# Layer 1 of a four-layer convolution kernel with three engines in fixed order, layer 2's first weights made in layer 0, and the last statistics from sums of two terms

## The chip, the cores and the metric

The kernel runs on one core of one Trainium2 chip. The metric is device time in microseconds (us) of one execution of the whole program. Every figure for a kernel is a median of its runs; beside it stands the range. Each result was correct against the reference. A submission runs its kernels and the kernel before in turn on one chip, so ratios are taken inside a submission: a ratio is the mean time of one kernel's fast runs over that of the other's of the same rounds, so it is not quite the ratio of the medians that are quoted.

In the lines of the profiler and in the recorded texts PE is TensorE (the matmuls), PEld its weight loads, DVE VectorE, ACT ScalarE and POOL GpSimd; L574 is line 574 of the kernel. A hole is idle time of TensorE between two matmuls. A half-clock stretch is a piece, 3.41 us or twice that unless said otherwise, in which the trace shows the granted TensorE clock at 0.50.

## The reference, cut to what matters

Input is x of 16 images, 256 channels, 28 x 28 pixels (784 per image and channel), in float32. Four layers follow each other.

```python
# layer 0: y = batchnorm(conv3x3(sign(x), sign(w))) + x            (statistics over all images)

# layer 1, per image, no statistics over images inside:
residual = prelu(x, a_alpha1)
z  = sign(x + a_move)
y  = prelu(bn(conv3x3(z, a_w)), a_alpha2)
g  = sigmoid(relu(mean(s*x + (1-s)*y) @ w1.T + b1) @ w2.T + b2)    # gate: one number per channel
y  = bn(g * y * residual) + residual
u  = prelu(bn(conv1x1(sign(y + f_move), f_w)), f_alpha2)
g2 = sigmoid(relu(mean(s2*y + (1-s2)*u) @ w1'.T + b1') @ w2'.T + b2')
x  = bn(g2 * u) + y

# layer 2 begins with statistics of that x over ALL images and pixels:
m, v = mean(x), var(x)
out  = sign(batchnorm(x))        # then conv3x3 with sign(w1) * mean(|w1|), and so on
# ... (rest of layer 2)
# layer 3: attention over the 784 pixels of each image, plus x
```

Two things matter. In layer 1 each image has a chain: 3x3 convolution, gate, product, 1x1 convolution, second gate, sum. Only the images are independent of each other. And layer 2 can't begin before the last image's x is in its statistics.

Of the kernel before, what the change touches and what calls it, by code (L numbers as in the profile page):

```python
# [64 lines left out]
def conv_seq_kernel(ctx: ExitStack, tc: tile.TileContext, d: dict, out: bass.AP):  # L65
# [78 lines left out]
    def norm(name, moments, gamma, beta, sf=None):  # L144
# [14 lines left out]
        r = rsqrt(name, v, half)  # L159
        tt(c, m, r, ALU.mult)  # L160
# [27 lines left out]
    def sign_weights(pool, dst, src, total, acc, stage=("st", 2), spare_dve=False, tmp=None, ab_tag="rn"):  # L188
# [9 lines left out]
        def sign(k, g):  # L198
            st = sts[k, g]
            n = CHUNKS.index((k, g))  # L200
            if n == 5:
                A.activation(dst[1], st, AF.Sign, saturate=False)
                return
            sg = tmp.tile([P, 3, 256], BF16, tag="t1", name="sg", bufs=2)
            A.activation(sg, st, AF.Sign, saturate=False)
            V.scalar_tensor_tensor(dst[0][:, n], sg[:, :, P:], PACK, sg[:, :, 0:P], ALU.mult, ALU.add)  # L206

        def add_up(k, g):
            st = sts.pop((k, g))
            if spare_dve:  # L210
                ab = st[:, 0, :]
                A.activation(st, st, AF.Abs)
                nc.gpsimd.tensor_tensor(ab, ab, st[:, 1, :], ALU.add)
                nc.gpsimd.tensor_tensor(ab, ab, st[:, 2, :], ALU.add)
            else:
                ab = tmp.tile([P, 256], F32, tag=ab_tag, name="ab", bufs=4 if ab_tag == "rn" else 2)
                V.tensor_reduce(ab, st.rearrange("p t o -> p o t"), AX.X, ALU.add, apply_absolute_value=True)
# [116 lines left out]
    with tc.tile_pool(name="ps_conv", bufs=3, space=PSUM) as psc, \  # L334
# [13 lines left out]
        with tc.tile_pool(name="ph1", bufs=1) as ph:  # L348
# [47 lines left out]
            def w1_step(k, c):  # L396
                sts = []

                def load():
                    sts.append(ph.tile([P, 3, 256], F32, tag="st", name="st", bufs=2))  # L400
# [18 lines left out]
            def fw_step():  # L419
                sts = []  # L420

                def load():
                    sts.append(ph.tile([P, 3, 256], F32, tag="st", name="stf", bufs=2))
# [46 lines left out]
            steps = load_ahead(steps, 2) + [x.work for x in sums_] + [constants]  # L470
# [17 lines left out]
            sc0, bi0 = norm("l0", mom, pv("g0"), pv("b0"), sf0)  # L488
            zb1 = tt(vtile("zb1"), bi0, pv("a_move"), ALU.add)
            nbi0 = combine("nbi0", bi0, -1.0)  # L490
            tt(mix_c[:, 0], pv("a_scale"), bi0, ALU.mult)

# [43 lines left out]
            def enter(b):  # L536

                sx = sums_of(b + 1)[0][:, 0]
                for k in range(2):
                    x = xs[b][:, k, :]  # L540
                    V.scalar_tensor_tensor(
                        x, ns[b][:, k, :], sc0[:, k:k + 1], x, ALU.mult, ALU.add, accum_out=sx[:, k:k + 1]
                    )
                    A.activation(inner(pads[b % 2], k), img(x), AF.Sign, bias=zb1[:, k:k + 1], saturate=False)

            def transform(b):
# [4 lines left out]
                terms = (  # L551
                    (e0, e1, ALU.subtract), (o0, e1, ALU.add), (e1, o0, ALU.subtract), (o0, o1, ALU.subtract)
                )
                for pair in ((1, 2), (0, 3)):
                    for k in range(2) if b == 0 else (slice(0, 2),):
                        for u in pair:
                            x, y, op = terms[u]
                            tt(vs[:, b % 2, u, k], x[:, k], y[:, k], op)

            def residual(b):  # L560

                for k in range(2):
                    x = xs[b][:, k, :]
                    r = relu_neg(x, nbi0[:, k:k + 1])
                    V.scalar_tensor_tensor(x, r, ra1[:, k:k + 1], x, ALU.mult, ALU.add)  # L565
# [15 lines left out]

            ys, us = {}, {}
# [7 lines left out]
            def sum_pair(b, mo):  # L590

                ps = pairs.pop((b, mo, True))
                t1, uv = temp("t1"), ph.tile([P, 2, HN], F32, tag="uv", name="uv", bufs=2)
                A.activation(t1, ps[:, 0, :HN], AF.Identity, bias=c1[:, mo:mo + 1], scale=s1[:, mo:mo + 1])
                for i, s in enumerate((s1, ns1)):
                    V.scalar_tensor_tensor(uv[:, i], ps[:, 1, :HN], s[:, mo:mo + 1], t1, ALU.mult, ALU.add)  # L596
                pairs[b, mo] = uv

            def rows_out(b, mo):
                ps = pairs.pop((b, mo, False))  # L600
                uv = pairs.pop((b, mo))
# [8 lines left out]
                pairs[b, mo] = relu_neg(y)  # L610

            def prelu_out(b, mo):
# [6 lines left out]
            def gates_hidden(t):  # L619
# [5 lines left out]
                tt(p, p, r, ALU.add)  # L625
                h = hidden[t % 3]
                for g, ps in enumerate(hidden_sums(p)):
# [15 lines left out]
            def branch1_a(b, g):  # L643
                for k in range(2):
                    y = ys[b, k]
                    if b == B - 1 and k == 1:
                        V.tensor_scalar(y, y, g[:, k:k + 1], 1.0, ALU.mult, ALU.add)
                    else:
                        A.activation(y, y, AF.Identity, bias=ones, scale=g[:, k:k + 1])

            def branch1_b(b):

                sv = sums_of(b + 2)[0][:, 1]
                room_x2(b)
                z2[b] = ph.tile([P, 2, N], FR, tag="z2", name=f"z2_{b}", bufs=1)
                for k in range(2):
                    v = x2[b][:, k, :]
# [696 lines left out]
```

## The kernel before: the parts that the change touches

Channels lie on the 128 partitions in two halves (`k` for input, `mo` for output). The 3x3 convolution of layer 1 is made of four products per pair of rows (`u` from 0 to 3), each of 12 matmuls. `conv_ps()` gives one of three PSUM buffers in rotation. Only TensorE's order is fixed by hand; VectorE and ScalarE are ordered by a scheduler that takes the order of the program text as a priority.

```python
with tc.manual_schedule(engines={ET.PE}):
    for b in range(B + 2):
        now, one, two, ahead = b < B, 0 <= b - 1 < B, 0 <= b - 2 < B, b + 1 < B
        if now:
            for i, u in enumerate((1, 2)):
                conv_pair(b, 0, i, u)            # TensorE: 24 matmuls
        ...
        if one or two:
            h = gates_hidden(b)                  # gate of b-1, second gate of b-2: "hid" on TensorE
        if now:
            sum_pair(b, 0)
            conv_pair(b, 0, 0, 0)
        if ahead:
            enter(b + 1)                         # next x: n * scale + x, and its signs
        if one or two:
            g = gates(h)                         # "gate" on TensorE
        if now:
            conv_pair(b, 0, 1, 3)
        ...
        if one:
            branch1_a(b - 1, g[:, 0])            # y * gate + 1
            branch1_b(b - 1)                     # times residual; z = its signs
        if now:
            rows_out(b, 0)                       # frees a PSUM buffer
        if two:
            branch2(b - 2, g[:, 1])              # x = u * gate + v, sums, squares, store
        if now:
            for i, u in enumerate((1, 2)):
                conv_pair(b, 1, i, u)
            prelu_out(b, 0)
        ...
        if ahead:
            transform(b + 1)                     # sums of rows for the next image's products
        if one:
            conv1x1(b - 1)                       # TensorE: 16 matmuls, two PSUM buffers
        if late:
            late()                               # a step that makes weights of layer 2
        if now:
            sum_pair(b, 1)
            for i, u in enumerate((0, 3)):
                conv_pair(b, 1, i, u)
        if one:
            unit_a(b - 1)                        # reads the result of the 1x1 convolution
        if ahead:
            residual(b + 1)
        if now:
            rows_out(b, 1)
        if one:
            unit_b(b - 1)                        # its sum is an input of the next "hid"
        if now:
            prelu_out(b, 1)
        late = steps.pop(0)() if b >= 2 and steps else None
```

The weights of layers 0 and 2 are used as signs, packed two to a number, and a matmul with a column of ones ("sumabs") gives the mean of their absolute values. One step does both:

```python
def sign(k, g):
    ...
    sg = tmp.tile([P, 3, 256], BF16, tag="t1", name="sg", bufs=2)
    A.activation(sg, st, AF.Sign, saturate=False)
    V.scalar_tensor_tensor(dst[0][:, n], sg[:, :, P:], PACK, sg[:, :, 0:P], ALU.mult, ALU.add)

def add_up(k, g):                       # the other form, on ScalarE and GpSimd, is cut
    st = sts.pop((k, g))
    ...
    V.tensor_reduce(ab, st.rearrange("p t o -> p o t"), AX.X, ALU.add, apply_absolute_value=True)
    return lambda: total_up(k, g, ab)   # 4 "sumabs" matmuls on TensorE, one step later

def both(first, second):
    return [Step(f.load, lambda f=f, s=s: (f.work(), s.work())[1]) for f, s in zip(first, second)]
```

After the last image, `moments1` adds up `sum_x2` and `sum_sq`, the sums of x and of (x + shift) squared per image, and only then does layer 2's scale and shift follow. `keep_busy(n)` issues n matmuls whose result is not used, so that TensorE's clock stays up.

## Time and profile before

| | before |
|---|---|
| median of 3 runs, us | 1184.69 (1183.12 to 1186.47) |
| layer 0 ends (TensorE's last product) | 157.7 |
| start of layer 1 | 7.5 |
| loop of layer 1, first product to last | 390.3 |
| tail: to the first product of layer 2 | 26.4 |
| first half image of layer 2 | 6.9 |

The rows of the table come from the starts of TensorE's instructions in the trace; they cut the time a little differently from the prediction's stages. The execution of before that was profiled took 1187.65 us, more than any of the three runs in the table.

On the page of the kernel before, these are the chain of work that ended last (share of the span by engine) and the group of the layer 1 products (busy time and mean ns of one, then the idle time of the engine just ahead of them and what ended most of it):

```profile
PE 62%; DVE 16%; ACT 4%; issue 2%; DMA 2%; DVEq 0%; ACTq 0%
L573 PE MATMUL cv<-vs,w 128*128 128x392 f32 x1536 | 309.9, 361 | 8.3 <-ACT rn L533 6.8
```

TensorE is busy nearly all the time, yet only 62% of the chain runs through it, and 16% through VectorE: in part of the program TensorE is led by others. The products' own idle time is small, 8.3 us. The larger idle time stands in front of the tiny gate matmuls, and the prediction shows it.

### The profile page before, as it was taken

The page shows a single profiled execution, that of the slowest core. Times are in us where ns is not written, and L with a number is a line of the kernel's source. Part 1 is how long each engine was busy: PE and PEld are TensorE (multiplying, and loading weights), DVE is VectorE, ACT ScalarE, POOL GpSimd, SP SyncE. Part 2 cuts the span into 40 slices and gives each one's busy share as a digit, 9 for nine tenths or more (in the row PEclk, how much of TensorE's full clock was granted, in tenths as well). Part 3 has the DMA queues.
Part 4 walks back from the last instruction along what each step waited for, and adds up shares of the span by engine and source line. Part 5 has one row for each costly group of instructions (what it writes and reads, how often), then busy time and mean ns, then how long its engine had stood idle before and what let it go on. Part 6 is the DMA issues. An engine that isn't in the chain of part 4 may idle for free.

```text
span 1185.9 us, 15794 instructions
## 1 busy us (share of the span) xinstructions
PE 1129.0 (95%) x6069; PEld 954.7 (81%) x6075; DVE 794.7 (67%) x1410; ACT 714.2 (60%) x1053; POOL 146.0 (12%) x144
## 2 busy tenths in 40 slices
PE   6999999998999999999999999999999999999995
PEld 6999989988999999998699998999965555555542
DVE  3854378888788888865476665666673666676565
ACT  4644545666667766755655554555567667767742
POOL 2000000011010000000000000000004434424421
PEclk9999999999999999999999999999999999999998
DMA  7653431222223212100545000000002554554522
GB/s 283 205 170 124 139 108 55 82 82 82 82 85 106 83 69 77 60 28 28 217 150 215 1 1 1 1 1 1 1 28 82 137 146 108 156 154 114 141 82 84
DMA packets 25973, 111.63 MB, mean 94 GB/s; under 512 B 3554, under 2 KB 6308, under 8 KB 25892
## 3 DMA queue, kind: packets, MB, share of 16 engines
q1 hardware_dynamic: 20436, 80.85, 19.4%
q0 software_dynamic: 5456, 29.71, 8.7%
q8 instruction: 50, 0.82, 0.3%
q14 instruction: 31, 0.25, 0.1%
HBM read 65.59 MB, written 44.96 MB: 93 GB/s over the span
## 4 chain that ended last, share of the span: by engine, by line
PE 62%; DVE 16%; ACT 4%; issue 2%; DMA 2%; DVEq 0%; ACTq 0%
PE cv L252 20%; PE cv L573 12%; PE sc L1014 7%; PE av L1035 6%; PE mi L999 4%; PE sm L1075 4%; DVE vs L103 2%; PE unused L346 2%; PE cv L271 2%; PE mi L1085 2%; PE cv L670 2%; DMA xs<-in_x_dram 2%; DVE y L606 2%; DVE uv L596 2%; DVE xs L565 1%
## 5 line engine op out<-in xcount | busy, mean ns | idle before, releaser
L573 PE MATMUL cv<-vs,w 128*128 128x392 f32 x1536 | 309.9, 361 | 8.3 <-ACT rn L533 6.8
L252 PE MATMUL cv<-fpads,wpk 128*128 128x392 f32 x1440 | 294.3, 357 | 10.9 <-DVE wpk L206 9.9
L573 PEld LDWEIGHTS cv<-vs,w 128*128 128x128 f32 x1536 | 293.0, 194 | 13.5 <-ACT rn L533 9.5
L252 PEld LDWEIGHTS cv<-fpads,wpk 128*128 128x128 f32 x1440 | 272.2, 192 | 15.7 <-issue 8.9
L1018 ACT ACTIVATE es<-sc 112x784 f32<-112x784 f32 x112 | 87.3, 821 | 74.7 <-PE sc L1014 74.5
L850 DVE SCALAR_TENSOR_TENSOR p<-r,r,cv 128x392 f32<-128x392 f32 x128 | 78.6, 614 | 79.7 <-ACT r L847 79.7
L252 PE MATMUL cv<-fpads,wpl 128*128 128x392 f32 x576 | 124.8, 352 | 0.0
L252 PEld LDWEIGHTS cv<-fpads,wpl 128*128 128x128 f32 x576 | 108.8, 190 | 0.6
L263 ACT ACTIVATE t<-cv,rounding 128x392 f32<-128x392 f32 x96 | 56.2, 585 | 87.2 <-PE cv L252 84.8
L1014 PE MATMUL sc<-q,k 64*112 64x392 f32 x448 | 90.4, 518 | 2.2 <-DVE k L1006 1.5
L264 DVE TENSOR_SCALAR uv<-t 128x392 fp32r<-128x392 f32 x96 | 35.0, 364 | 82.8 <-ACT t L263 82.8
L847 ACT ACTIVATE r<-cv 128x784 f32<-128x784 f32 (+1 forms) x66 | 52.9, 804 | 60.1 <-PE cv L271 59.2
L1035 PE MATMUL av<-es,va 112*64 112x392 f32 x448 | 80.8, 499 | 0.0
L1014 PEld LDWEIGHTS sc<-q,k 64*112 64x112 f32 x448 | 36.4, 175 | 43.6 <-issue 18.7
L1028 POOL TENSOR_TENSOR sum<-sum,es 112x784 f32<-112x784 f32 x32 | 68.4, 2139 | 2.5
L1035 PEld LDWEIGHTS av<-es,va 112*64 112x64 f32 x448 | 29.6, 136 | 47.4 <-issue 44.6
L103 DVE TENSOR_TENSOR vs<-pad 128x840 fp32r<-128x840 bf16 (+1 forms) x68 | 65.3, 985 | 2.4 <-PE cv L573 1.5
L1006 DVE COPY k<-mi 64x784 f32<-64x784 f32 x16 | 15.6, 976 | 65.1 <-ACT q L1005 65.1
L477 ACT CAST n<-cv 128x784 int16<-128x784 f32 x32 | 26.0, 812 | 55.1 <-DVE l_parts L476 24.2
L1075 PEld LDWEIGHTS sm<-wv,p 128*112 128x112 f32 x448 | 46.7, 178 | 5.0 <-issue 2.6
L1089 DVE TENSOR_TENSOR p<-mi,p 128x784 f32<-128x784 f32 x30 | 29.2, 974 | 31.5 <-PE mi L1085 31.1
L271 PE MATMUL cv<-uv,unpack 128*128 128x392 f32 x192 | 49.9, 341 | 0.0
(235 smaller groups left out, 1669.1 us busy)
## 6 DMA issues: line engine op xcount, KB each, us to landing
xs<-in_x_dram SPq DMA_DIRECT2D x32, 784.0 KB, 4.6
x2d<-x POOLq DMA_DIRECT2D x16, 784.0 KB, 3.8
xd<-p SPq DMA_DIRECT2D x16, 784.0 KB, 3.3
out_dram<-p SPq DMA_DIRECT2D x15, 784.0 KB, 5.2
p<-x2d SPq DMA_DIRECT2D x13, 784.0 KB, 7.6
p<-x2d POOLq DMA_DIRECT2D x13, 784.0 KB, 9.1
n0d<-n POOLq DMA_DIRECT2D x16, 392.0 KB, 2.7
n<-n0d SPq DMA_DIRECT2D x16, 392.0 KB, 3.1
```

The lines of the kernel that those rows point to most:

```text
L103: V.tensor_tensor(o, a, b, op)
L252: T.matmul(pss[j][:, mo, :HN].rearrange("p (a b) -> p a b", b=S), lhsT=lhsT, rhs=pads[:, j // 2 % 2, k, r:r + HR, c:c + S], start=start, s ...
L263: A.activation(r, pss[j][:, 0, :HN], AF.Identity, bias=rounding, scale=1.0 / PACK)
L271: T.matmul(pss[j][:, mo, :HN], lhsT=unpack[mo], rhs=bs[j], start=False, stop=True, skip_group_check=(mo == 0))
L573: T.matmul(ps.rearrange("p (a b) -> p a b", b=S), lhsT=w[:, k, c, u, mo * P:(mo + 1) * P], rhs=vs[:, b % 2, u, k, :, c:c + S], start=(n == 0),
L847: A.activation(r[:, mo], ps[:, mo, :HN], AF.Relu, scale=-1.0)
L850: V.scalar_tensor_tensor(p, r[:, mo], beta[:, mo:mo + 1], ps[:, mo, :HN], ALU.mult, ALU.add)
L1014: T.matmul(ps[:MC, h, :HN], lhsT=k_[rows, c * MC:(c + 1) * MC], rhs=qs[b][rows], start=True, stop=True)
L1018: A.activation(e, ps[:MC, :, :HN], AF.Exp, scale=0.125)
L1028: (V if late else nc.gpsimd).tensor_tensor(sums[b, late], sums[b, late], e, ALU.add)
L1035: T.matmul(ps[64 * h:64 * h + 64, :HN], lhsT=w, rhs=e[:, h, :], start=start, stop=stop)
L1075: T.matmul(ps[:MC, c * 64:(c + 1) * 64], lhsT=x[b][:, k, c * MC:(c + 1) * MC], rhs=wv[:, k, :], start=(k == 0), stop=(k == 1),)
```

## The change

Three things are done together.

1. **Layer 1.** VectorE and ScalarE get a fixed order too, not only TensorE. The iteration is cut elsewhere: the gate's two matmuls stand one product later, the 1x1 convolution stands at the end of TensorE's iteration, and the passes that read its result move to the start of the next iteration. So does the second prelu.
2. **Layer 2's first weights** (five steps of signs, packing and absolute sums) are made in layer 0, whose VectorE and ScalarE have room, and no longer in layer 1. They get buffers of their own. The other weight steps of layer 0 are spread out between them.
3. **The tail.** For the last image, x = v + g u. Its sum and its sum of squares are formed from sums of v and u before the gate g is known, so the two passes that make x no longer stand ahead of the shift and scale of layer 2. The load of the square root's table is pulled ahead.

The diff is long; this is its core, with cuts marked by "...".

```diff
-            sg = tmp.tile([P, 3, 256], BF16, tag="t1", name="sg", bufs=2)
+            sg = tmp.tile([P, 3, 256], BF16, tag="sg", name="sg", bufs=1)
...
-            steps = load_ahead(steps, 2) + [x.work for x in sums_] + [constants]
+            w2a = [packed_weights(wpool, tag="wa2"), None]
+            signs2, sums2 = sign_weights(xpool, w2a, d["w2a"], sf1, pss, ("x2", 3), tmp=ph)
+            steps = load_ahead(steps + both(signs2, sums2)[:5], 2)
+            for i, x in enumerate(sums_):
+                steps.insert(2 * i + 1, x.work)
+            steps.insert(13, constants)
...
-            with tc.manual_schedule(engines={ET.PE}):
-                for b in range(B + 2):
...
+            def iteration(b):
+                ahead, one, two = b + 1 < B, b >= 1, b >= 2
...
+                for i, u in enumerate((1, 2)):
+                    conv_pair(b, 0, i, u)
+                if two:
+                    unit_u(b - 2, 0)
+                if one:
+                    prelu_a(b - 1, 1)
+                if two:
+                    unit_r(b - 2, 0)
+                    unit_u(b - 2, 1)
+                    unit_r(b - 2, 1)
...
+                conv_pair(b, 0, 0, 0)
+                h = hidden_a(b) if one else None
...
+                if one:
+                    h = hidden_b(b, h)
...
+                conv_pair(b, 0, 1, 3)
+                rows_out(b, 0)
+                if one:
+                    g = gates(h)
...
+                for i, u in enumerate((1, 2)):
+                    conv_pair(b, 1, i, u)
...
+                if ahead:
+                    transform(b + 1, 0)
+                    transform(b + 1, 3)
+                    for i, u in enumerate((0, 3)):
+                        conv_pair(b, 1, i, u)
+                    rows_out(b, 1)
+                    if one:
+                        conv1x1(b - 1)
...
+            with tc.manual_schedule(engines={ET.PE, ET.DVE, ET.Activation}):
+                sc0, bi0 = norm("l0", mom, pv("g0"), pv("b0"), sf0, first)
...
+                squares(x2[b][:, 0, :], shift[:, 0:1], sum_vv[:, 0:1])
...
+                for k in range(2):
+                    products(x2[b][:, k, :], shift[:, k:k + 1], us[b, k][0], sum_uv[:, k:k + 1])
+                squares(us[b, 0][0], 0.0, sum_uu[:, 0:1])
...
+                def moments1():
+                    tt(d1, su, g, ALU.mult)
+                    tt(q1, sum_uu, g, ALU.mult)
...
+                sg1, bg1 = norm("l2a", moments1, pv("g1"), pv("b1"))
+                for k in range(2):
+                    branch2(b, k, g)
...
-            keep_busy(20)
-            sg1, bg1 = norm("l2a", moments1, pv("g1"), pv("b1"))
+            keep_busy(12)
```

## The prediction

> **What bounds the kernel now.** I read the page's totals first, then the table of stages, then who waits for whom in layer 1, then one iteration in order of time.
>
> ```profile
> PE 1129.0 (95%) x6069; PEld 954.7 (81%) x6075; DVE 794.7 (67%) x1410; ACT 714.2 (60%) x1053; POOL 146.0 (12%) x144
> ```
>
> TensorE is the fullest engine, but that row is an average over stages. The table of stages (length, busy time and count of PE, weight loads, DVE, ACT, POOL, granted clock, DMA share, GB/s) splits it:
>
> ```profile
> 13.00:158.00 145.00, 143.81 (x751) 141.13 (x753) 73.69 (x190) 73.89 (x121) 8.32 (x15) 1.00 0.48 168
> 158.00:165.20 7.20, 6.50 (x31) 2.80 (x31) 5.48 (x22) 3.20 (x6) 0.54 (x1) 1.00 0.44 135
> 165.20:366.00 200.80, 185.05 (x961) 181.16 (x962) 167.09 (x312) 131.75 (x182) 13.53 (x16) 0.96 0.24 81
> 366.00:555.80 189.80, 181.19 (x961) 175.25 (x961) 151.01 (x285) 124.16 (x177) 5.41 (x12) 0.99 0.18 63
> 555.80:581.90 26.10, 23.31 (x107) 12.32 (x107) 15.12 (x44) 14.44 (x25) 2.11 (x6) 0.93 0.22 81
> 581.90:717.00 135.10, 133.67 (x715) 131.76 (x716) 84.83 (x167) 75.78 (x99) 0.00 (x0) 1.00 0.29 113
> ```
>
> Layer 0 (13 to 158) and layer 2 (from 582) are PE streams without holes. Layer 1 (165.2 to 555.8, 390.6 us) has PE holes, DVE is over 80% busy there, and the clock is below 1. The stage after it, the tail of layer 1, takes 26 us in which PE mostly runs filler. Who waits for whom in layer 1 (total, times, longest):
>
> ```profile
> PEld hid L507 <- DVE g L103: 21.3, 14, 2.7
> PE hid L507 <- DVE g L103: 16.7, 14, 2.3
> ```
>
> PE stands still before the tiny gate product "hid", because VectorE gets to its input late. One such place on PE, with clock of the three 3.4 us pieces around it:
>
> ```profile
> 345.97 0.61 PE L507 MATMUL hid<-g,se 128*128 128x2 f32 x4 [1.82 <-DVE g L103]
> 346.44 3.77 PE L573 MATMUL cv<-vs,w 128*128 128x392 f32 x12
> 350.01 0.74 PE L637 MATMUL gate<-hidden,se 128*128 128x2 f32 x4
> ```
> ```profile
> 343.70:347.10 3.40, 1.58 (x11) 1.22 (x10) 2.75 (x7) 1.15 (x3) 0.00 (x0) 1.00 0.00 0
> 347.10:350.50 3.40, 3.40 (x13) 3.40 (x12) 0.00 (x0) 0.03 (x1) 0.00 (x0) 0.50 0.00 0
> 350.50:353.90 3.40, 3.40 (x19) 3.39 (x20) 2.87 (x6) 2.15 (x3) 0.41 (x1) 1.00 0.00 0
> ```
>
> After the hole, twelve matmuls take 3.6 us where they take 2.36 elsewhere: the hole is paid twice, once as idle time and once as 3.4 us at half clock. Half-clock stretches in the layer 1 loop begin at 190, 217, 245, 296, 347 and 514: six, each worth about 1.7 us.
>
> **What the Trainium skill says.** "TensorE: Matmul & The Clock Gate", Part 1, says the clock halves after an idle window of about 3.4 us and recovers after a busy one. The trace agrees on half and on 3.4 us, but here 1.82 us of idleness, less than a window, was enough. The same page, "LDWEIGHTS", gives columns / 1.2, 107 ns for 128 columns; the trace has 194 ns for these f32 weights, and matmuls of 392 columns follow each other every 0.192 us, so I use 0.192. "VectorE: DVE Perf Modes", the perf-mode tier table, keeps an fp32 op on two tensors at one element a cycle; the trace agrees: 784 elements follow each other every 0.955 us. "ScalarE: Activation LUTs", "What ACT_TABLE_LOAD costs", gives 1283 ns; the trace has 1283 ns before the last statistics' square root.
>
> **Loop of layer 1.** The arithmetic per image does not change; order does. PE's floor for an iteration, from one without holes (489.4 to 502.4): 36 matmuls 6.90, hid 0.47, 12 matmuls 2.36, gate 0.36, 48 matmuls 9.20, the 1x1 convolution 2.90: 22.19 us. DVE needs 12 passes of 784 and 4 transforms at 0.955, 8 passes of 392 at 0.54, and small ones: 20.1 us. ACT needs about 16. So PE is the bound if the order lets it be. Sixteen iterations less one 1x1 convolution (2.90) and one gate (0.36) are 351.8. Before's 390.6 is that plus 24.0 of holes (summed from PE's gaps), 10.2 of half clock, 2.3 for five groups of sumabs products (0.46 each) and 2.3 that I can't place.
>
> I laid the new order by hand, PE's first matmul of an iteration at 0, with durations from the trace. DVE: the second prelu at 0.7, enter and two unit passes to 4.5, so hid's input is there at 5.1; PE wants it at 6.9 (slack 1.8). On ACT, hidden stands ahead of the second residual ReLU, so DVE waits until 9.05; from there 12.2 us of DVE work end at 21.3 with rows_out, which frees the PSUM tile that PE writes next at 22.19 (slack 0.9). The three PSUM buffers rotate so that the other tiles are free over 3 us early. x and n are loaded an iteration ahead (4.6 us to land). So no wait in the steady state. In iteration 15 the 1x1 convolution was moved ahead of the last pair; its second input is ready at 16.45 and wanted at 15.4: 1.1 us lost. Loop: 351.8 + 2.3 + 1.1 + 0.5 for what I overlook = 355.7, **34.9 us less**.
>
> **Start of layer 1.** The first pass over x begins before the shift is ready, and one sign and the first half transforms follow without the second: first matmul near 164.2, not 165.2: **1.0 less**.
>
> **Layer 0.** Five sign-and-sum steps for layer 2's weights move here. DVE and ACT have room (half busy), but their sumabs products lie in a full PE stream: 5 x 0.46 = 2.3 more (halves take 4.79 with them, 4.33 without). Spreading the w1 steps should give back about 1.5 of the 2.1 lost in halves of 5.24 and 5.26. The sign buffer has one copy instead of two: 0.4 more at the start. Sum **+1.2**.
>
> **Tail.** Before, from the last row pass to the first matmul of layer 2, 26.0. Its end in order of time:
>
> ```profile
> 580.68 0.16 DVE L103 TENSOR_TENSOR l2a_c<-vec,l2a_c 128x2 f32<-128x2 f32 x1
> 581.00 1.36 ACT L820 ACTIVATE fpads<-x,l2a_c,l2a_r 128x420 fp32r<-128x420 f32 x2 [1.41 <-issue]
> ...
> 581.84 0.43 PE L252 MATMUL cv<-fpads,wpk 128*128 128x392 f32 x1
> ```
>
> The new tail takes image 15's statistics from sums of u and v, so the last update of x (two passes, 1.9) need not precede them, and the table load is pulled ahead. By hand: gate 5.6, z 9.4, u 13.8, second hid 16.6, two product passes to 18.5, gates 19.4, last square 19.9, about fourteen small steps of 0.1 to 0.2 with the square root, shift ready at 23.0 instead of 25.0. That is 2.0 gained. **But it may not reach PE.** In the built program the first sign of layer 2 waits for a count of VectorE that is only reached by the second last update of x (its buffers take over layer 1's memory), and on POOL the store of that x stands ahead of clearing the pads. So: updates to 24.9, store issued to 25.5 (0.53 before), two memsets to 26.1, first matmul near 26.3. Fillers end near 23.9 (26 of 0.22), so PE idles 2.4 us and probably falls to half clock: 0.7 x 1.7. Sum **+1.5**.
>
> Sum: 1184.7 - 34.9 - 1.0 + 1.2 + 1.5 = 1151.5.
>
> **Rivals.** (a) DVE becomes the bound: 20.1 us of work plus two fixed waits fill almost all of 22.2. If each handover costs 0.1 more, rows_out comes after 22.19 and each iteration grows by 0.5: 1160. The dense stretches of before, where passes follow at 0.955, speak against it. (b) Small new holes trip the clock: at 3 places, 3 x (1 + 1.7) = 8 us more, 1160. For it: six of before's holes did it; against: holes under 0.8 us never did. (c) The fixed order is worse than the scheduler's on ACT, because an engine in order stops for one late input: the period stays near 23.5 as in before's second half: 1173. Against: slack by hand is 0.9 or more everywhere. (d) The tail gains its 2.0 after all and layer 0 costs nothing: 1147.
>
> **Range and chances.** (a) to (c) lengthen, (d) shortens; all moderately likely. 1143 to 1163 should hold 8 in 10. Two per cent is 1161: faster 0.88, same 0.11, slower 0.01 (all engines' work is the same or less).
>
> **What would show it.** Right: iterations of 22.2 us; no wait before hid; clock 1.00 in the loop; ACT's first sign of layer 2 starting only after the second last update, with PE idle ahead of it; halves of 4.79 in 11 places of layer 0. Wrong if: holes before the first matmuls of an iteration (DVE bound), half-clock stretches in the loop, a tail under 25 us or over 29, or layer 0 longer by more than 3 us.

## The result, and the profile after

The changed kernel took 1153.01 us (1151.66 to 1154.10, 4 runs), the kernel before in the same rounds 1185.49 us (1183.12 to 1186.47, 4 runs). The ratio is 0.9728, with a 95% interval of 0.9708 to 0.9748. The prediction was 1151.5 us, the range 1143 to 1163.

By the same cut as above, from the two traces:

| stage, us | before | after | difference | predicted |
|---|---|---|---|---|
| layer 0 ends | 157.73 | 164.70 | +6.97 | +1.2 |
| start of layer 1 | 7.47 | 6.64 | -0.83 | -1.0 |
| loop of layer 1 | 390.26 | 348.93 | -41.33 | -34.9 |
| tail | 26.38 | 27.03 | +0.65 | } +1.5 |
| first half image of layer 2 | 6.92 | 8.62 | +1.70 | } |
| all that follows | 597.1 | 596.0 | -1.1 | 0 |
| span of the profiled run | 1185.9 | 1151.9 | -34.0 | -33.2 |

The sum came out within a microsecond, but two terms in it did not: the loop gained 6.4 us more than predicted, and layer 0 lost 5.8 us more. The two cancel, so that the total came out this close is luck. In the last row but one, the trace of before has a half-clock stretch at 889.8 us and that of after has none there.

These are the same two places of the page, after:

```profile
PE 79%; issue 5%; DVE 4%; ACT 2%; POOL 0%; POOLq 0%; ACTq 0%; DVEq 0%
L574 PE MATMUL cv<-vs,w 128*128 128x392 f32 x1536 | 301.4, 354 | 0.0
```

The share of TensorE in the chain rose from 62% to 79%, that of VectorE fell from 16% to 4%, and the layer 1 products have no idle time ahead of them at all.

The table of stages, after (us, then busy time and count of PE, weight loads, DVE, ACT, POOL, then granted clock, DMA share and GB/s):

```profile
13.00:164.70 151.70, 146.82 (x771) 144.73 (x771) 81.27 (x205) 77.36 (x125) 8.35 (x15) 0.99 0.48 168
171.34:520.60 349.26, 348.57 (x1901) 346.38 (x1902) 312.54 (x586) 248.56 (x348) 8.50 (x18) 1.00 0.22 78
520.60:547.30 26.70, 21.57 (x100) 11.55 (x99) 19.26 (x64) 15.54 (x29) 1.60 (x4) 0.94 0.10 32
```

In the loop TensorE is busy for 348.57 of 349.26 us at a clock of 1.00. VectorE, at 312.54, is 89% busy, and the list of waits shows none of TensorE for it. Layer 0, in contrast, now has 4.9 us in which TensorE is idle, where it had 1.2.

One iteration of the loop in order of time, TensorE alone:

```profile
299.80 7.00 PE L574 MATMUL cv<-vs,w 128*128 128x392 f32 x36
306.63 0.50 PE L506 MATMUL hid<-g,se 128*128 128x2 f32 x4
309.35 0.50 PE L649 MATMUL gate<-hidden,se 128*128 128x2 f32 x4
...
321.76 1.49 PE L574 MATMUL cv<-vs,w 128*128 128x392 f32 x7
```

No line shows an idle time in brackets: each piece follows the one before it. From 299.80 to 321.76 the iteration takes 21.96 us.

In layer 0 something new shows (all engines, order of time; the brackets give the idle time before an instruction and what ended it):

```profile
92.23 1.61 ACT L359 ACTIVATE fpads<-xs 128x784 fp32r<-128x784 f32 x2
93.74 0.83 ACT L207 ACTIVATE sg<-st 128x768 bf16<-128x768 f32 x1
94.60 0.56 DVE L208 SCALAR_TENSOR_TENSOR wpk<-sg 128x384 fp32r<-128x384 bf16 x1 [3.17 <-ACT sg L207]
95.07 1.02 DVE L213 TENSOR_REDUCE ab<-st 128x256 f32<-128x768 f32 x1
96.15 0.61 PE L219 MATMUL sumabs<-ones,ab 128*128 128x1 f32 x4 [2.45 <-DVE ab L213]
```

Read it from below. TensorE stood still for 2.45 us before the sumabs matmuls, because VectorE's sum of absolute values (ab) came late. That sum needs only the loaded weights, but in VectorE's fixed order it stands behind the packing (wpk), and VectorE waited 3.17 us for the signs (sg), which on ScalarE stand behind the signs of the next image (fpads). The trace has three such holes, 2.45, 1.12 and 1.12 us, and a half-clock stretch begins at 97.5, right after the first.

The end of the tail, after:

```profile
543.75 0.16 DVE L103 TENSOR_TENSOR l2a_c<-vec,l2a_c 128x2 f32<-128x2 f32 x1
545.98 2.53 ACT L933 ACTIVATE fpads<-x,l2a_c,l2a_r 128x420 fp32r<-128x420 f32 x4 [3.32 <-DVE x L710]
546.12 0.53 POOL L716 DMA_DIRECT2D x2d<-x  x1 [13.78 <-DVE x L710]
...
547.30 5.00 PE L248 MATMUL cv<-fpads,wpk 128*128 128x392 f32 x16 [1.96 <-POOL fpads L90]
```

The shift of layer 2 (l2a_c) is ready at 543.91, but its first sign starts at 545.98: it waits for the second of the two updates of the last x, which ends at 545.81 (the prediction named the one before that). The store of that x precedes the clearing of the pads on GpSimd, so TensorE begins at 547.30 after 1.96 us of idleness. The half clock that was feared came too: from 548.1 to 551.5 the granted clock is 0.50. That it falls there is chance: e8 below has the same tail, also of 27.03 us, but in its trace the half clock falls on the filler (532.8), and the first half image of layer 2 takes 7.18 us for 8.62.

### The profile page after: what moved, and what is told of

It reads as the page before. It is cut to its first block, busy times and chain, and to the rows that moved or that the text cites. A ratio compares the mean times of both kernels' runs of the same rounds, so it can differ in the third digit from the quotient of the medians.

```text
span 1151.9 us, 15800 instructions
## 1 busy us (share of the span) xinstructions
PE 1113.7 (97%) x6062; PEld 948.5 (82%) x6067; DVE 801.2 (70%) x1430; ACT 711.5 (62%) x1051; POOL 135.8 (12%) x134
## 4 chain that ended last, share of the span: by engine, by line
PE 79%; issue 5%; DVE 4%; ACT 2%; POOL 0%; POOLq 0%; ACTq 0%; DVEq 0%
PE cv L248 24%; PE cv L574 23%; PE sc L1127 7%; PE av L1148 7%; PE mi L1112 4%; PE sm L1188 4%; PE cv L678 3%; PE cv L267 2%; PE mi L1198 2%; PE unused L342 1%; PE sm L1148 1%; ACT fpads L933 1%; DVE r L1173 0%; PE hid L506 0%; PE gate L649 0%
## 5 line engine op out<-in xcount | busy, mean ns | idle before, releaser
L248 PE MATMUL cv<-fpads,wpk 128*128 128x392 f32 x1440 | 297.9, 360 | 11.3 <-DVE wpk L208 8.9
L574 PE MATMUL cv<-vs,w 128*128 128x392 f32 x1536 | 301.4, 354 | 0.0
L574 PEld LDWEIGHTS cv<-vs,w 128*128 128x128 f32 x1536 | 287.4, 190 | 1.6 <-issue 0.3
L716 POOL DMA_DIRECT2D x2d<-x x16 | 8.5, 533 | 366.8 <-DVE x L710 304.0
```

Of the source, the lines that this page charges most:

```text
L248: T.matmul(pss[j][:, mo, :HN].rearrange("p (a b) -> p a b", b=S), lhsT=lhsT, rhs=pads[:, j // 2 % 2, k, r:r + HR, c:c + S], start=start, s ...
L574: T.matmul(ps.rearrange("p (a b) -> p a b", b=S), lhsT=w[:, k, c, u, mo * P:(mo + 1) * P], rhs=vs[:, b % 2, u, k, :, c:c + S], start=(n == 0),
```

## The experiments

Twelve kernels were run. All outputs are right. Kernels are compared only within the same rounds. The kernel before took 1184.28 us (e1, e4, e5, e6), 1184.45 (e3, e7, e8, e9), 1186.08 (p1, p2 and the best version) and 1184.48 (p3). Names that begin with "e" start from the changed kernel, those with "p" from the kernel before.

Stages are read from one trace per kernel, and they vary. With the changed code of layer 0 untouched (the changed kernel, e3 to e7 and e9), layer 0 ends between 164.30 and 166.54; with that of before (before, p1 to p3), between 155.70 and 158.34. So a difference of 2 us in that stage shows nothing unless its place is found in the trace.

### Layer 0: the sum of absolute values ahead of the packing

```diff
-            st = sts.pop((k, g))
+            st = sts[k, g]
...
-        return [Step(f.load, lambda f=f, s=s: (f.work(), s.work())[1]) for f, s in zip(first, second)]
+        return [Step(f.load, lambda f=f, s=s: (s.work(), f.work())[0]) for f, s in zip(first, second)]
```

> Edit: in each step that prepares sign weights, the sum of absolute values is taken before the sign is packed, no longer after it; nothing else. Theory: layer 0 of the changed kernel is 7.0 us longer than before (last product at 164.7 instead of 157.7) because PE's tiny sumabs products stand in its fixed order ahead of the next half, and the sum they need is behind a pack on DVE that waits for a sign on ACT that stands behind the pads of the next image: three holes of 2.45, 1.0 and 1.0 us, and one half-clock stretch at 97.5. With the sum first the holes vanish: layer 0 ends near 158.4, the three holes of 0.7, 0.3 and 0.3 in layer 2 go as well, time near 1145.5. Rival: the weights arrive late (their load is issued late on SP): the holes stay, time 1153.

Measured: 1143.17 us (1142.65 to 1146.22), ratio 0.9647 (0.9627 to 0.9667). Layer 0 ends at 158.02 in place of 164.70, and the first convolution of layer 2, which uses the same helper, is 2.04 us shorter from its first product to its last (144.17 for 146.21). The same step in order of time:

```profile
91.56 1.03 DVE L213 TENSOR_REDUCE ab<-st 128x256 f32<-128x768 f32 x1
93.76 0.50 PE L219 MATMUL sumabs<-ones,ab 128*128 128x1 f32 x4
93.95 0.83 ACT L207 ACTIVATE sg<-st 128x768 bf16<-128x768 f32 x1
94.81 0.56 DVE L208 SCALAR_TENSOR_TENSOR wpk<-sg 128x384 fp32r<-128x384 bf16 x1 [2.23 <-ACT sg L207]
```

The sum is done at 92.59, TensorE takes it at 93.76 without a wait, and VectorE's wait for the signs is still there but holds up nothing. This is shown: of the 7.0 us that layer 0 lost, 6.7 were the order of two instructions.

### The preparation of layer 2's weights back into layer 1

```diff
-            steps = load_ahead(steps + both(signs2, sums2)[:5], 2)
+            steps = load_ahead(steps, 2)
...
+                late, prep = None, load_ahead(both(signs2, sums2)[:5], 1)
                 for b in range(B):
                     iteration(b)
+                    if late:
+                        late()
+                    late = prep.pop(0)() if b >= 2 and prep else None
```

> Edit: the five steps that prepare layer 2's first weights are back in layer 1, one at the end of each of iterations 2 to 6, in fixed order (the row sums' buffer and the weights' buffer trade places for room). Theory: layer 0 ends near 156 (no holes before sumabs, none for the first weights either) instead of 164.7; layer 1 has 0.9 us of slack on DVE and each step brings 1.6 us of DVE work and 0.46 of PE, so five iterations grow by about 1 us each: loop 354 instead of 349. Time near 1149, less than the changed kernel. Rival: DVE is full in layer 1[...]: loop 365 or more, time above 1158, so that the move paid.

Measured: 1146.12 us (1145.46 to 1146.30), ratio 0.9674 (0.9658 to 0.9691). Layer 0 ends at 154.99 and the loop is 351.78, only 2.85 longer, without a hole. So moving the preparation, as it was done, cost more (9.7 us in layer 0) than it brought in the loop (2.85); the new loop would have carried it. Even with the sum first (e1) the five steps cost layer 0 3.03 us (158.02 for 154.99), no less than the 2.85 they save in the loop, so no run shows a gain from moving them. Layer 0 without the preparation is also 2.7 us shorter than in the trace of before. Of that, 2.2 are four halves of 4.49 to 5.26 us, which with the other weight steps spread out take 4.33 or so.

### The tail: taking the locks off

Two things were believed to stand between the shift and layer 2's first product: the buffer that makes the first sign wait for the second update, and the store ahead of the pads. In e3, only the buffer is changed; in e4, also the store.

```diff
 # e3 and e4
-                u = full("yu", f"u{b}_{mo}", 6)
+                u = full("yu", f"u{b}_{mo}", 6) if b < B - 1 else uvs[:, mo].rearrange("p i n -> p (i n)")
 # e4 only: the store of the last x is issued after the first weight step of layer 2
-                if k == 1:
+                if k == 1 and b < B - 1:
                     nc.gpsimd.dma_start(out=x2d[b], in_=x2[b])
```

> Edit: only the first of the two locks off (u of image 15 kept in the free buffer); the store of image 15 still stands ahead of the clearing of the pads on POOL. Theory: the first sign of layer 2 now starts near 544.1 instead of 546.0, but PE still waits for the pads, which are cleared after the store is issued: first matmul near 547.3 as in the changed kernel, time 1153. Rival: the sign alone was the lock: first matmul near 545.4, time 1149.5.

> Edit: u of image 15 is kept in the free buffer of the row sums, so that layer 2's pads no longer take over memory that the second last update of x reads; and the store of image 15 is issued after the pads are cleared. Theory: the shift is ready at 543.9 but the first sign waits until the update ends at 545.7 and the pads until the store is issued at 546.6. With both locks off the first matmul of layer 2 starts right after the fillers, near 545.4 instead of 547.3 (26.7 us after the first stage's last matmul begins becomes about 25.1), and without the hole there is no half clock at the start of layer 2 (1.7 us): time near 1149.4. Rival: the start is set by something else, a load or the fillers: no change, 1153.

Measured: e3 1152.31 us (1151.17 to 1153.27), ratio 0.9724; e4 1152.52 us (1151.07 to 1152.70), ratio 0.9724. Neither separates from the changed kernel's 0.9728. In e3 the scheduler by itself put the clearing of the pads ahead of the store, so that both locks were off there as well: the two can't be told apart by these runs. That e4 brought nothing has a reason that its trace shows:

```profile
539.18 7.46 PE L342 MATMUL unused<-idle 128*128 128x512 bf16 x26
543.76 2.54 ACT L933 ACTIVATE fpads<-x,l2a_c,l2a_r 128x420 fp32r<-128x420 f32 x4 [1.41 <-DMA st<-in_w2a_dram]
546.28 0.92 PE L248 MATMUL cv<-fpads,wpk 128*128 128x392 f32 x3
```

The first sign now starts at 543.76, 2.2 us earlier than in the changed kernel. But a half-clock stretch begins at 539.9 and falls on the 26 matmuls that keep TensorE busy; they take 7.46 us (5.77 in the changed kernel), and the first product of layer 2 follows right behind the last of them at 546.28, 2.5 us after the first sign began. With fewer fillers, in the last experiment, that takes 0.8 us: the filler had become the bound. The first half image of layer 2 then ran at full clock (6.99 for 8.62).

### The tail: more filler

```diff
-            keep_busy(12)
+            keep_busy(22)
```

> Edit: 22 fillers instead of 12 before layer 2. Theory: the half-clock stretch at 548 comes from the 2.0 us hole between the last filler and the first matmul of layer 2. With ten fillers more (2.2 us) the hole is gone, the start is later by 0 to 0.3 us, and the first two halves take 6.9 instead of 8.6 us: time near 1151.5. Rival: the stretch has another cause (the earlier holes around the gates): no gain, 1153.

Measured: 1154.20 us (1151.68 to 1155.22), ratio 0.9736 (0.9712 to 0.9760). It is a miss. The first half image of layer 2 fell from 8.62 to 6.99, but the tail grew from 27.03 to 28.55, for the half-clock stretch now falls on the filler (540.0). It follows a window of 3.41 us with 1.43 us of idle time, the two holes around the gate (0.82 and 0.61), as in e4 and e8; in the trace of the changed kernel these two lie in different windows. So this stretch has the rival's cause, and more filler behind the gate can't prevent it; the one at 548.1 in the changed kernel does follow the hole of 1.96 us, as the theory had it. Against e8, whose 12 are hit in the same way (27.03 and 7.18), ten more cost 1.3 us.

### The tail: the statistics as before

The sums of two terms are replaced by the old form (update x, square it, then `moments1`), in the new fixed order.

```diff
-                def moments1():
-                    tt(d1, su, g, ALU.mult)
...
+                for k in range(2):
+                    branch2(b, k, g)
+                for k in range(2):
+                    squares2(b, k)
+                def moments1():
+                    V.tensor_reduce(m, sum_x2, AX.X, ALU.add)
...
```

> Edit: image 15's statistics taken as before the change, from the finished x (two updates, two squares, then mean and variance), in the fixed order and with the square root's table still loaded ahead; the order of everything else kept. Theory: the new statistics bring the shift 1 to 2 us earlier but put the last update after it, where the first sign of layer 2 waits for it. With the old ones the shift is ready about 24.4 us after the last convolution product (23.3 now), but nothing stands behind it: the first matmul comes about 25.3 us after, against 27.0 now, and time is 1150 to 1152. Rival: the sums of two terms give the 2.0 us they were made for: undone, time is 1155.

Measured: 1152.39 us (1151.37 to 1152.87), ratio 0.9724 (0.9704 to 0.9745). In its trace the tail is 25.38 and the first half image 7.00, together 32.38 against 35.65 in the changed kernel. But here the half clock falls on the filler (540.1), and there on layer 2; against e8, where it falls on the filler too (34.21), the new statistics, with what they drag along, cost that stage 1.8 us. The kernel's time shows neither a cost nor a gain: layer 0 of this trace is 1.7 us longer (166.38), as its half clock after the first hole lasts 6.83 us for 3.41. The rival's 1155 did not come, so the third part of the change as it was built brought nothing that the runs show.

### The fixed order of VectorE and ScalarE alone

```diff
-            with tc.manual_schedule(engines={ET.PE, ET.DVE, ET.Activation}):
+            with tc.manual_schedule(engines={ET.PE}):
```

> Edit: in layer 1 only PE is in fixed order, as before the change; VectorE and ScalarE are ordered by the scheduler again; code and all else as in the changed kernel. Theory: it is the fixed order of DVE and ACT that brings g to the hid product in time. Given back to the scheduler, iterations take about 23.5 us again (as in the second half of layer 1 before) instead of 22.0, with holes before hid: loop 373 instead of 349, time near 1177. Rival: the rewritten order of the code and the 1x1 convolution at the end of the iteration suffice: loop 349 to 355, time 1153 to 1159.

Measured: 1157.13 us (1155.03 to 1160.30), ratio 0.9761 (0.9742 to 0.9779). My theory fell, and the rival was right: the loop takes 350.33, only 1.4 more. The scheduler, given the new text of the iteration as priority, finds an order nearly as good for the loop. The fixed order is worth 1.4 us in the loop, 0.9 at the start of layer 1 (7.54 for 6.64) and 4.5 in the tail (31.48 for 27.03). The last figure is an upper one: the profile is of the slowest of the four executions (1160.30), with 10.2 us at half clock in its tail.

### The place of the 1x1 convolution in the new loop

```diff
+                    if one:
+                        conv1x1(b - 1)
                     for i, u in enumerate((0, 3)):
                         conv_pair(b, 1, i, u)
                     rows_out(b, 1)
-                    if one:
-                        conv1x1(b - 1)
```

> Edit: in every iteration the 1x1 convolution stands ahead of the last pair of products on PE, as before the change, the rest in the new order. Theory from the hand-laid order: its second input is ready about 1.05 us after PE wants it, and the PSUM tiles rotate the other way, so that the next iteration's first tile is freed by a ScalarE pass that now stands behind one that waits for the last pair: some 2.9 us more. Iterations of 25.5 to 26 instead of 22.0, several half-clock stretches, time 1200 to 1220. Rival: the place of the 1x1 convolution does not matter: time within 5 us of 1153.

Measured: 1189.35 us (1189.13 to 1190.99), ratio 1.0038 (1.0021 to 1.0055). The loop takes 386.29, so 37 of its 41 us are gone. TensorE in one iteration:

```profile
306.68 2.42 PE L678 MATMUL cv<-z,fw 128*128 128x392 f32 x12 [0.60 <-ACT z L670]
308.94 4.71 PE L574 MATMUL cv<-vs,w 128*128 128x392 f32 x24
314.90 7.09 PE L574 MATMUL cv<-vs,w 128*128 128x392 f32 x36 [1.25 <-DVE y L614]
```

The 1x1 convolution comes too early for its input (0.60), and the next image's first products wait 1.25 us for a PSUM buffer that VectorE's row pass (y) frees. Over the loop these are 9.1 and 17.5 us. The remaining 11 of the 37 us lie beside the holes: at each stop a few products take 0.28 to 0.36 us to the next start, the hole not counted, where 0.18 to 0.19 is usual. Over the loop such steps add 14.3 us, in the changed kernel 3.2. No half-clock stretch fell into this loop; the theory expected several, and a ScalarE pass in place of VectorE's, hence its 1200 to 1220 us.

### One part alone, in the kernel before

Three kernels build the new cut step by step in the old loop, with the scheduler's order and the preparation left in the loop. The first moves the gate's matmuls one product later; the second also puts the 1x1 convolution last on TensorE; the third also reads its result in the next iteration.

```diff
 # p1, p2, p3 (the second gate matmul likewise, after conv_pair(b, 0, 1, 3))
-                    if one or two:
-                        h = gates_hidden(b)
                     if now:
                         sum_pair(b, 0)
                         conv_pair(b, 0, 0, 0)
+                    if one or two:
+                        h = gates_hidden(b)
 # p2, p3
-                    if one:
-                        conv1x1(b - 1)          # ahead of the last pair
...
+                    if one:
+                        conv1x1(b - 1)          # behind it
 # p3 only: behind the first pair of products of the iteration
+                    if two:
+                        unit_a(b - 2)
+                        unit_b(b - 2)
...
-                    if one:
-                        unit_a(b - 1)
...
-                    if one:
-                        unit_b(b - 1)
```

> The kernel before, with one thing changed: in the order of TensorE the first matmul of the gate stands one product group later and the second one too (one group is 9 matmuls of the convolution times two, some 7 us). The scheduler still orders VectorE and ScalarE. Theory (the idle time of TensorE in the old loop is mainly its waiting for the sums of the gate, with the half clock that follows from it): the holes before that matmul, up to 2.3 us, go, and most of the half-clock stretches of the loop with them; the loop of layer 1 shrinks from 390 us by 15 to 30 us and the kernel takes 1155 to 1170 us. Rival (the loop is bound by VectorE and ScalarE as the scheduler orders them, and a later gate makes the next stage late): a new hole elsewhere, at the z tiles of the 1x1 convolution or the sums of the pair, and a loop over 380 us, the kernel over 1174 us.

> The kernel before with the gate's two matmuls later, as in the run beside it, and the 1x1 convolution after the last pair of products in place of ahead of it. VectorE and ScalarE still in the scheduler's order, and the reading of the 1x1's result still in the same iteration. Theory (in the changed kernel the place of the 1x1 convolution was worth 37 us of the loop, its fixed order on the other engines 1.4 us): the two places on TensorE alone bring most of the gain, the loop falls to 355 to 370 us, the kernel to 1145 to 1165 us. Rival (the place of the 1x1 convolution is worth much only because the new order moves the reading of its result into the next iteration; here the gate waits for that reading): holes before the gate's first matmul or at the products after the 1x1, and a loop over 375 us.

> The kernel before with the gate's matmuls later and the 1x1 convolution after the last pair, as in the run before this one, and one thing more: the result of the 1x1 convolution is read (both passes over PSUM and the sum) in the next iteration, behind that one's first pair of products, as the changed kernel does. VectorE and ScalarE stay in the scheduler's order, and the preparation of layer 2's weights stays in the loop. Theory (the gain of the loop is this cut of the iteration: order on TensorE alone only moved the hole to the next wait, because the chain from the 1x1's result to the gate had to fit into one iteration): no hole of 1.2 us or more in the iterations of the middle of the loop, the loop of layer 1 355 to 372 us in place of 382 to 390, the kernel 1155 to 1172 us. Rival (the rest of the new order on VectorE and ScalarE is needed as well: the passes of the next image ahead of the prelu and so on): holes stay at the gate or at the sums of the pair, the loop over 376 us and the kernel over 1176 us.

(A slip in the first of these texts: a product group is 12 matmuls, about 2.4 us.)

| | us | ratio to before | loop of layer 1 |
|---|---|---|---|
| p1 | 1188.61 (1186.46 to 1189.15) | 1.0018 (1.0002 to 1.0033) | 385.82 |
| p2 | 1191.97 (1188.57 to 1194.12) | 1.0058 (1.0043 to 1.0074) | 382.14 |
| p3 | 1171.96 (1171.05 to 1172.63) | 0.9888 (0.9871 to 0.9904) | 364.98 |

For p1 and p2 my theory fell and the rival was right. Who waits for whom on TensorE in the loop (total, times, longest), first p1, then p2, then p3:

```profile
PE cv L573 <- DVE uv L596: 17.4, 13, 1.4
PE hid L507 <- DVE g L103: 6.2, 6, 2.4
```
```profile
PE hid L507 <- DVE g L103: 15.3, 13, 1.6
PE cv L573 <- ACT rn L533: 7.9, 14, 0.6
```
```profile
PE hid L507 <- DVE g L103: 12.5, 13, 1.3
```

In p1 the wait before the gate fell from 16.7 to 6.2 us, and a wait for the sums of the pair (uv, which free a PSUM buffer) of 17.4 us took its place. In p2 it is again the gate, 15.3, with 7.9 for a buffer that the reading of the 1x1's result frees. In each the sum of the holes stays at 23 to 25 us (24.4 in before). Only when the reading of that result is allowed to fall into the next iteration, in p3, do the holes halve and the loop falls by 17 us at once. The rival has its share here too: 12.5 us of waiting before "hid" remain, with a hole of 1.3 where the theory allowed none of 1.2.

Two things blur the table. In p2 and p3 the last image's 1x1 convolution lies behind the last product, so that 2.9 us pass from the loop to the tail; on an equal cut p2 gains 5.2 us of loop, p3 22.4, and p3 still lacks 18.9: 12.8 of holes, 2.9 of preparation (e8), 1.7 of half clock, and 1.5 more. And the edit puts the second gate matmul of the last two iterations behind 14 fillers. In all three traces the last 1x1 convolution then waits 4.01 us for its input z, and the tails are 32.8, 38.4 and 36.2 us for 26.4. So the times of p1 and p2, the same as or a little above before, hide what little their loops gain.

### Putting the findings together

The changed kernel with the order of e1, both locks off as in e4, and 18 in place of 26 fillers:

```diff
 # the edits of e1 and of e4, and
-            keep_busy(12)
+            keep_busy(4)
```

> The changed kernel with the sum of absolute values ahead of the packing in layer 0 (worth 9 us in its own run), with both locks of the tail taken off (store of the last x after the first sign of layer 2; u of the last image in a buffer of its own) and 18 in place of 26 fillers on TensorE between the gate and layer 2. Theory: the fillers were what layer 2 waited for once the locks were off; with 8 fewer (2.3 us at their 0.287 us each of that run) layer 2 starts 1.5 to 2.5 us earlier than with 26 fillers, and the kernel takes about 1139.5 us, 1137.5 to 1141.5. Rival: fewer fillers leave TensorE idle so that the half clock falls on the start of layer 2 again (its first half 8.6 us in place of 7.0), and the kernel takes 1141 to 1143.5 us, the same as with the order of the sums alone.

Measured: 1141.40 us (1140.71 to 1142.42, 5 runs), ratio 0.9625 (0.9612 to 0.9639). It lies at the upper edge of what the theory gave, and inside the rival's band too, so the time alone does not decide; the trace does:

```profile
532.88 5.73 PE L342 MATMUL unused<-idle 128*128 128x512 bf16 x18
537.46 2.54 ACT L933 ACTIVATE fpads<-x,l2a_c,l2a_r 128x420 fp32r<-128x420 f32 x4 [1.41 <-DMA st<-in_w2a_dram]
538.30 5.99 PE L248 MATMUL cv<-fpads,wpk 128*128 128x392 f32 x30
```

The fillers end close to the first sign's first piece (a half-clock stretch falls on them here too, at 534.1), layer 2 starts 24.70 us after the last product (26.44 in e4, 27.00 in e1), and its first half image takes 6.95, not 8.6 as the rival had it. This is the fastest kernel. Its interval overlaps that of e1, so how much it gains over e1 in time is not settled; tail and first half image together are 4.0 us shorter in the traces.

## Why the prediction was right

The time was right, and the direction of each part. By its own steps:

- **What bounds the kernel: right.** The holes before "hid" and the half-clock stretches were what the loop could lose. After the change the loop has no hole over 0.1 us until its last iteration, and no half-clock stretch.
- **Loop: right in mechanism, the size was off by 6.4 us.** The prediction gave 355.7, the trace has 348.9. The floor of 22.19 us per iteration came from an iteration of before "without holes"; small delays were still in it (hid 0.47, now 0.36), and the new iteration takes 21.96. Sixteen of them, less the missing 1x1 convolution (2.86) and gate (0.36), are 348.1, against 351.8: 3.7 us. The 2.3 us that the prediction could not place, and carried over, did not come back. The lost time in iteration 15 was found where it was said, at the late second input of the 1x1 convolution: its hole is 0.69 us, and with the slow steps around it the stop costs 1.16, so the 1.1 stood. The reserve of 0.5 was not used. Together 6.5 of the 6.8.
- **Where the loop's gain comes from: more than the prediction said.** It ascribed it to "order" and expected the slack by hand to do. The experiments show which order. Moving the gate alone (p1) or also the 1x1 convolution (p2) only turned one wait into another of much the same total; putting the reading of the 1x1's result into the next iteration as well halved the holes (p3, 22.4 us of loop gained). The other half, the wait before "hid", goes with the rest of the new order: e8, which has it all and still prepares the weights in the loop, gains 38.5. Which piece of that rest does it no run shows. In the new order, taking the 1x1 convolution's place back costs 37 us (e9); and fixing VectorE and ScalarE is worth 1.4 us (e7). The parts need each other, so no sum of single effects can be given.
- **Start of layer 1: right,** 0.83 for 1.0.
- **Layer 0: wrong in size, +7.0 for +1.2,** by the prediction's own test ("longer by more than 3 us"). The terms of its sum were off by 1.6 and 0.7 us, against each other: spreading the steps with the single sign buffer gave 2.7 less (e8 against before), where -1.5 + 0.4 was written; the five steps cost 3.0 (e1 against e8), where 2.3 was written. What the sum lacked was a term for order: "DVE and ACT have room (half busy)" is true, and an engine in fixed order still stops for one late input. That was 6.7 us (e1): 4.7 of holes and the half-clock stretch behind them. The prediction named this very danger for layer 1, as rival (c), and did not look for it in layer 0.
- **Tail: right in mechanism,** +2.35 for +1.5 if the first half image of layer 2 is taken with it. The shift is ready 23.6 us after the last product, before 25.4: 1.8 earlier, for 2.0 predicted. The gain did not reach TensorE, by the wait for the update and the store that were named. The half clock, given 0.7, fell as named in this trace and on the filler in that of e8. What the prediction did not see is the next bound behind them: with the locks off, the filler holds layer 2 (e4), and only fewer fillers let the gain through (the last run).
- **The rivals.** (a) VectorE did not become the bound, although 89% busy. (b) holes did trip the clock, not in the loop but in layer 0 and the tail. What was put down against it, that holes under 0.8 us never did, misread before's trace: in its tail two of 0.58 and 0.61 us lie in one window, and half clock follows at 562.1. (c) did not happen in the loop. (d) was the reverse of what happened in layer 0.
- **A reading that was wrong and cost nothing:** the 194 ns of a weight load are the length of its record, not the time to the next load (see the last section); the sums used 0.192 us per product, which is measured.
- **Not predicted:** the 1.1 us in what follows, where before has a half-clock stretch at 889.8 and the changed kernel none. What such a stretch falls on depends on the phase of the clock's windows (see the last section), so it is not put down to the change.

## What to carry to other kernels

When an engine waits once per iteration, ask how far its result is from its reader around the whole loop: moving the waiting instruction alone passed the wait on here, moving the reader into the next iteration took half of it away, and the other half went with the rest of the new order. Work that is moved to a stage with room on its engines has to be ordered so that what the bound engine reads comes first, here the sum ahead of the packing; busy shares don't show that. And filler that keeps the clock up is itself on the path once what it covers gets shorter, so count it again after each gain. Before two tails are compared, see in both traces where the half clock falls.

## What the Trainium skill lacked or had wrong

- **"TensorE: Matmul & The Clock Gate", Part 1.** It says that the clock halves after an idle window of about 3.4 us and that these windows run freely, each 3413 ns. The traces agree on the free-running windows: the starts of before's half-clock stretches in the loop (190.1, 217.4, 244.7, 295.9, 347.1 and 514.3) lie 8, 8, 15, 15 and 49 times 3.413 us apart. But a window need not be idle. I added up TensorE's idle time inside each window of the loops of layer 1 in six kernels (before, after, p1, p2, p3, e9): each of the nine windows with 1.45 us or more of it was followed by half clock, none with 1.25 or less was, and of those between some were (1.26 in p3, 1.34 in before, 1.41 twice in p1) and some were not (1.28 in p2, 1.34 in before, seven of 1.35 to 1.41 in p1). The idle time is to be taken window by window: a hole of 2.02 us at 267.2 in before, which straddles two, was not followed by half clock, and holes of 1.25 us in most iterations of e9 never were. It does not decide alone, and the figures are for these loops: in the tails 1.09 us was enough in e3, and 1.92 was not in p1.
- **The same page, "LDWEIGHTS".** Its formula, columns / 1.2, gives 107 ns for 128 columns. The record of an f32 weight load is longer, 190 ns on average in layer 1 of the changed kernel, but that is no contradiction: before "hid" at 306.6 such loads are recorded at 189 to 192 ns each and start 0.110 and 0.111 us after one another, which agrees with the formula. The 0.191 us from one product of 392 columns to the next is thus not the pace of the loads as such; what sets it is open.
- **No page that I read** says that on an engine with instructions in fixed order a half busy engine can cost the bound one 6.7 us over five steps (e1), or that filler matmuls at half clock can become the bound (26 in 7.46 us, in e4).
